# The last token tile of z moved behind the FFN's second inner product, and the first blocks of W loaded at the first free buffer

## The chip, the cores and the metric

The kernel runs on one core of a Trainium2 chip. The metric is device time in microseconds of one execution, and the median over runs is compared. The profile is of one such execution.

## The reference, cut to what matters

```python
# x: (2, 1024, 2048), ctx: (2, 2048, 2048), float32
def fake_quant(x, scale, zp):
    q = clip(round(x / scale + zp), 0, 255)
    return (q - zp) * scale

x = x + fake_quant(layernorm(x)) @ fake_quant(ctx[b])            # first layer, per batch b
z = layernorm(x)
x = x + z @ W + bias + LoRA(z)                                   # second layer, "the FFN"
# LoRA(z): a gated mixture of 16 adapters of rank 32, chosen per group of
# 256 tokens, and a shared adapter of rank 32: (z @ A_eff.T) @ B_eff.T + (z @ A_sh.T) @ B_sh.T
```

W is 2048 x 2048. Each of the 2 batches has 1024 tokens, that is 8 token tiles of 128 (m = 0 to 7), or 4 groups of 256 (g = 0 to 3).

## The kernel before, in words

**Stages.** The two batches are computed one after the other, and each has two stages: the first layer (called xattn here) and the FFN. The residual y (x, then the result) stays in SBUF, one tile of two token tiles per group.

**First layer.** Its product is made in pairs (n, g): 512 output columns n by one token group g. `xattn_pair` (line 555) issues 32 bf16 matmuls of 512 columns (line 530, tile `pa`). Then `end` (line 547) on VectorE scales the sums and adds them to y, and `bn_stats` (line 551) takes the statistics of the new y for the second layernorm. The last column block is n = 3: its four pairs (3, 0) to (3, 3) end the first layer of the batch.

**z.** When pair (3, g) is done, token tiles 2g and 2g+1 of y are complete, and `prep_z` (line 622) makes z of one tile. VectorE does a chain of small operations on 128 x 1 columns (lines 334 to 358, with one square root on ScalarE, line 341). Then for each half of 1024 columns VectorE writes (y - mean) * rstd into the buffer `wk` (line 628), TensorE transposes it in two groups of four 128 x 128 blocks into PSUM (line 632, tile `ptz`), and ScalarE copies each group into the z buffers (line 633). `wk` has one place for each half, so half h of tile m+1 can be written only when half h of tile m is transposed. `ptz` shares a PSUM pool of two buffers (`ps_m`) with other small tiles. `group_z` (line 635) does the two tiles of a group and then writes z to a scratch in DRAM (`zs`, line 639, issued on ScalarE's queue).

**LoRA's first product.** `lora_ax` (line 642) multiplies two groups' z by the adapters: 64 matmuls of 256 columns on TensorE (line 648, tile `px`). It comes once for groups 0 and 1 and once for groups 2 and 3. `Delta` (line 658) spreads the second LoRA product (line 694, tile `pl`) over the FFN.

**FFN.** z @ W is done by two levels of Strassen's method in Winograd's form: 7 outer combinations (o, table OUTER), and in each 7 inner products (s, table INNER). One inner product (`product`, line 812) is 8 float32 matmul instructions of 512 columns on 256 tokens; the profile records each of them as two rows. Their sums collect in the PSUM chains `fu`, `fv` and `fw`, and `spread` (line 837) adds a chain to y on VectorE (line 852). The operands are blocks of z (names a.., buffers `lit`) and of W (names b.., buffers `big`) and sums and differences of them. `comb` (line 766) makes these: those of W on VectorE as 128 x 2048 operations, those of z on GpSimd (POOL) as 128 x 1024 operations, both with line 771 in the profile. For o = 0 the combinations are t1 = b12 - b11, t2 = b22 - t1, t3 = b22 - b12, s1 = a21 + a22, s2 = s1 - a11, s3 = a11 - a21. The blocks a11, a12, a21, a22 of o = 0 are sums over two groups of z, done on VectorE at line 1093; a21 and a22 are written over the z of group 1, so they wait until `px` and the write to `zs` have read it.

**Buffers.** `big` has 9 buffers, handed out by a first-in first-out list while the program is built. They hold the first layer's operands (four `c1T` buffers, one for each group, and two pairs for ctx), `wk`, and in the FFN the blocks of W. A load of W (line 752, on SyncE's queue, 1 MB each) waits until its buffer is free.

**What sets the order.** The Tile framework orders the instructions of each engine when the kernel is built, by the program's order and its own estimates. So an FFN matmul can stand between two transposes where the data allow it. On the chip the order of each engine is fixed, and each engine runs its own list in order.

**Around the change** (lines 1068 to 1113): the operands of o = 0 are loaded one by one while pairs (3, 0) to (3, 3) run; `group_z` of a group stands after the next pair; `group_z` of group 3, `lora_ax` of groups 2 and 3, and `Delta` stand ahead of the first FFN product in the program.

Of the kernel before, what the change touches and what calls it, by code (L numbers as in the profile page):

```python
# [15 lines left out]
ALU = mybir.AluOpType  # L16
# [82 lines left out]
def tile_quant_xattn_then_lora_ffn(  # L99
# [17 lines left out]
    nc = tc.nc  # L117
    B, S, D = x.shape
    KT = D // P
    MT = S // P  # L120
# [8 lines left out]
    MG = GT // P  # L129
# [15 lines left out]
    big = Bufs([const.tile([P, KQ, NB], F32, tag=f"big{i}", name=f"big{i}") for i in range(9)])  # L145
    lit = Bufs([const.tile([P, KQ, GT], F32, tag=f"lit{i}", name=f"lit{i}") for i in range(10)])
# [13 lines left out]
    zs = [  # L160
        [[dram.tile([P, KQ, GT], F32, tag=f"zs{b}{g}{q}", name=f"zs{b}{g}{q}") for q in range(4)] for g in range(GPB)]
        for b in range(B)
    ]
# [89 lines left out]
    for i, s in enumerate((x1_scale, x1_zp, x2_scale, x2_zp)):  # L253
# [16 lines left out]
        out=gate_b.rearrange("p b n -> p (b n)"), in_=gate.rearrange("b n -> (b n)").partition_broadcast(P)  # L270
# [82 lines left out]
    def norm_stats(stats, name):  # L353

        mean, ve = variance(stats, name)
        r0, t = end_norm(ve, root_of(ve, name), name)
        rstd = small.tile([P, 1], F32, tag="rstd", name=f"rstd_{name}")
        nc.vector.tensor_mul(rstd, r0, t)
        return mean, rstd

    def halves(buf):

        f = flat(buf)
        return f[:, 0:H], f[:, H : 2 * H]
# [190 lines left out]
    def xattn_pair(b, n, g, c1T, c2):  # L555
        p = Pair(b, n, g, c1T, c2)
        for j in range(MG):
            with tc.high_priority():
                p.begin(j)
            p.products(j, range(KT))  # L560
        summed = p.end()
        p.stats()
        return summed
# [47 lines left out]
    def lora_b_step(b, n):  # L611

        st, sf = gated(f"b{b}_{n}")
        for c in range(NC):
            for i in range(2):
                nc.sync.dma_start(
                    out=bd[b][i::2, i, ds(c * RC, RC), ds(n * NB, NB)],
                    in_=sf[ds(c * GP + i * (GP // 2), GP // 2), :],
                )
        q2b.give(st)  # L620

    def prep_z(b, m, zq, wk):

        nm = f"{b}_{m}"
        g, tok = m // MG, ds((m % MG) * P, P)
        mean, rstd = norm_stats(st2[:, m], f"z{nm}")
        for h, t in enumerate(halves(wk)):
            nc.vector.tensor_scalar(t, y[g][:, m % MG, ds(h * H, H)], mean, rstd, ALU.subtract, ALU.mult)
            for u in range(2):
                pt = ps_m.tile([P, KQ, P], F32, tag="pm", name=f"ptz_{nm}_{h}_{u}")  # L630
                for k in range(KQ):
                    nc.tensor.transpose(pt[:, k, :], t[:, ds((4 * u + k) * P, P)], ident)  # L632
                nc.scalar.copy(zq[2 * h + u][:, :, tok], pt)

    def group_z(b, g, wk, zq):
        for j in range(MG):
            prep_z(b, g * MG + j, zq, wk)
        for q in range(4):
            nc.scalar.dma_start(out=zs[b][g][q], in_=zq[q])
        return zq  # L640

    def lora_ax(b, pr, zqs):

        px = ps_m.tile([P, GT], F32, tag="pm", name=f"px_{b}_{pr}")
        for k in range(KT):
            for i in range(2):
                g = 2 * pr + i
                nc.tensor.matmul(  # L648
                    px[i * 2 * R : (i + 1) * 2 * R, :],
                    acat[:, k, ds(3 * pr + i, 2), :].rearrange("p s r -> p (s r)"),  # L650
                    zqs[i][k // KQ][:, k % KQ, :],
                    start=(k == 0),
                    stop=(k == KT - 1),
                    skip_group_check=True,
                )
        nc.scalar.copy(axT[:, pr, :], px)
# [149 lines left out]
    def acc_tag(o, chain):  # L806

        return "delta" if chain == "v" and o > 3 else f"acc{(o + (chain != 'u')) % 2}"
# [3 lines left out]
    def product(b, o, s, ops, chains):  # L812

        an, bn, chain, opens, (i, j) = INNER[s]
        if opens:
            if chain == "u" and b + 1 == B and o == NO - 1:

                chains[chain] = [ps_m.tile([P, NB], F32, tag="pm", name=f"f{chain}_{b}_{o}{m}") for m in range(MG)]
            else:
                ps = ps_acc.tile([P, MG, NB], F32, tag=acc_tag(o, chain), name=f"f{chain}_{b}_{o}")  # L820
                chains[chain] = [ps[:, m, :] for m in range(MG)]
                whole[chain] = ps
        ps = chains[chain]
        ends = not any(c == chain and not op for _, _, c, op, _ in INNER[s + 1 :])
        at, bt = ops.t[an], ops.t[bn]
        for m in range(MG):
            for k in range(KQ):
                nc.tensor.matmul(  # L828
                    ps[m],
                    at[:, k, ds(m * P, P)],  # L830
                    bt[:, k, :],
                    start=(opens and k == 0),
                    stop=(ends and k == KQ - 1),
                    skip_group_check=True,
                )
# [17 lines left out]
            if done:  # L853
                nc.scalar.dma_start(out=out[b, ds(g * GT, GT), cols].rearrange("(j p) n -> p j n", p=P), in_=yp)

    def ffn(b, ops, meanwhile):

        delta = Delta(b)
        for o in range(NO):
            nxt = Operands(b, o + 1) if o + 1 < NO else None  # L860
            chains = {}
            for s in range(len(INNER)):
                product(b, o, s, ops, chains)
                if s in OWN:
                    OWN[s](ops)
                if nxt and s in AHEAD:
                    AHEAD[s](nxt)
                spread(b, o, s, chains)
                if s in (1, 4):
                    delta.step()  # L870
                added = line.last
                if nxt:
                    for name in BLOCKS.get(s, ()):
                        nxt.block(name)
                for name in DROP.get(s, ()):
                    ops.drop(name)
                if nxt:
                    for name in BEGIN.get(s, ()):
                        nxt.load(name)
                with tc.issue_after(added):  # L880
                    meanwhile(o, s)
            ops = nxt
# [20 lines left out]
    wk = big.take()  # L903
# [6 lines left out]
    def close_c2(n):  # L910
        for t in c2b.pop(n):
            big.give(t)
# [107 lines left out]
    for b in range(B):  # L1020
# [45 lines left out]
        close_c2(2)  # L1066
        bp.give(colt.pop(2))
        first = Operands(b, 0)
        first.load("b11")
        zqs = {}  # L1070
        for g in range(GPB):
            xattn_pair(b, 3, g, c1T, c2[3])
            big.give(c1T_bufs[g])
            if g == 0:
                first.block("b11")
                first.load("b12")
            elif g == 1:
                first.block("b12")
                first.comb("t1", "b12", "b11", ALU.subtract)
            elif g == 2:  # L1080
                first.load("b22")
            if g < 3:
                lora_b_step(b, g + 1)
            if g > 0:
                zqs[g - 1] = [lit.take() for _ in range(4)]
                group_z(b, g - 1, wk, zqs[g - 1])
            if g == 2:

                lora_ax(b, 0, [zqs[0], zqs[1]])
                for i in range(2):  # L1090
                    for j in range(2):
                        to = lit.take() if i == 0 else zqs[i][j]
                        nc.vector.tensor_add(to, zqs[i][j], zqs[i][2 + j])
                        first.t[f"a{i + 1}{j + 1}"] = to
                for t in (*zqs[0], *zqs[1][2:]):
                    lit.give(t)
        close_c2(3)
        bp.give(colt.pop(3))
        first.block("b22")
        z3 = [big.take() for _ in range(2)]  # L1100
        zqs[3] = [t[:, :, ds(h * GT, GT)] for t in z3 for h in range(2)]
        first.load("b21")
        group_z(b, 3, wk, zqs[3])
        big.give(wk)
        first.block("b21")
        first.comb("t2", "b22", "t1", ALU.subtract)
        first.comb("s1", "a21", "a22", ALU.add)
        first.comb("s2", "s1", "a11", ALU.subtract)
        lora_ax(b, 1, [zqs[2], zqs[3]])
        for t in zqs[2]:  # L1110
            lit.give(t)
        for t in z3:
            big.give(t)

        state = {"x": 0}

        def meanwhile(o, s):
# [41 lines left out]
            if s == len(INNER) - 1:  # L1159
# [5 lines left out]
                for m in range(4, MT):  # L1165
                    load_x(nb, m, slice(H, D))

        ffn(b, first, meanwhile)
        if b + 1 < B:
            c1T_bufs, c1T, wk = state["c1b"], state["c1T"], state["wk"]  # L1170

# [52 lines left out]
```

## Time and profile before

| | us |
|---|---|
| median of 3 runs (lowest to highest) | 1082.38 (1082.28 to 1082.62) |
| time of the profiled execution | 1082.56 |
| its span, first to last instruction | 1080.8 |
| TensorE (PE) busy | 1054.6 |
| VectorE (DVE) busy | 766.6 |
| ScalarE (ACT) busy | 247.4 |
| GpSimd (POOL) busy | 253.8 |

A row of the timeline has its start and its length in us, both on the profile's own clock, then the engine, the line of the code, the operation, the tile written and the tiles read, and in brackets the idle time of the engine just before it with what ended it. A row can merge several instructions (x8). The chain of waits lists the work that ended last, in order of time: start, length, what. In the first batch the last pair of the first layer ends at 179.5 us and the FFN runs until about 515 us. In the second batch the same pair ends at 708.1 us. The mean granted clock of TensorE is 1.00.

### The profile page before, as it was taken

The page shows a single profiled execution, that of the slowest core. Times are in us where ns is not written, and L with a number is a line of the kernel's source. Part 1 is how long each engine was busy: PE and PEld are TensorE (multiplying, and loading weights), DVE is VectorE, ACT ScalarE, POOL GpSimd, SP SyncE. Part 2 cuts the span into 40 slices and gives each one's busy share as a digit, 9 for nine tenths or more (in the row PEclk, how much of TensorE's full clock was granted, in tenths as well). Part 3 has the DMA queues.
Part 4 walks back from the last instruction along what each step waited for, and adds up shares of the span by engine and source line. Part 5 has one row for each costly group of instructions (what it writes and reads, how often), then busy time and mean ns, then how long its engine had stood idle before and what let it go on. Part 6 is the DMA issues. An engine that isn't in the chain of part 4 may idle for free.

```text
span 1080.8 us, 10609 instructions
## 1 busy us (share of the span) xinstructions
PE 1054.6 (98%) x3932; PEld 489.8 (45%) x3932; DVE 766.6 (71%) x949; ACT 247.4 (23%) x351; POOL 253.8 (23%) x104
## 2 busy tenths in 40 slices
PE   5999999999999999999999999999999999999998
PEld 2443345544444444444444444554444444444443
DVE  7986867578877676677859655674969667756851
ACT  5866133210000000001675741331000000000000
POOL 0000003032435302533000000032244531253600
PEclk9999999999999999999999999999999999999999
DMA  9979645788798476699673292559889874748611
GB/s 341 381 196 308 190 176 190 256 316 295 263 339 324 160 264 217 191 372 321 230 246 119 98 266 103 198 210 360 294 269 297 288 269 148 264 146 301 214 39 58
DMA packets 119228, 257.15 MB, mean 238 GB/s; under 512 B 11272, under 2 KB 15496, under 8 KB 118152
## 3 DMA queue, kind: packets, MB, share of 16 engines
q1 hardware_dynamic: 98688, 215.05, 58.4%
q10 hardware_dynamic: 20168, 40.38, 10.7%
q0 software_dynamic: 320, 1.05, 0.4%
q8 instruction: 31, 0.51, 0.2%
q14 instruction: 21, 0.17, 0.1%
HBM read 220.79 MB, written 37.75 MB: 239 GB/s over the span
## 4 chain that ended last, share of the span: by engine, by line
PE 83%; DVE 8%; DMA 4%; ACT 3%; issue 1%; SPq 0%; ACTq 0%
PE fu L828 34%; PE fv L828 17%; PE pa L530 12%; PE fw L828 9%; PE pl L694 3%; PE px L648 3%; PE ptz L632 2%; DMA lit<-in_ctx_dram 2%; DVE st L551 2%; DVE st L383 1%; ACT q2b L458 1%; DVE y L547 1%; ACT big L412 1%; DVE big L771 1%; PE pg_b L574 1%
## 5 line engine op out<-in xcount | busy, mean ns | idle before, releaser
L828 PE MATMUL fu<-big,lit 128*128 128x512 f32 x896 | 395.3, 593 | 0.0
L828 PEld LDWEIGHTS fu<-big,lit 128*128 128x128 f32 x896 | 168.6, 190 | 206.3 <-issue 204.9
L530 PE MATMUL pa<-big,big 128*128 128x512 bf16 x1024 | 237.1, 381 | 7.3 <-ACT pa L526 3.4
L771 POOL TENSOR_TENSOR lit<-lit,lit 128x1024 f32<-128x1024 f32 x56 | 164.7, 2950 | 189.7 <-PE fw L828 74.6
L828 PE MATMUL fv<-big,lit 128*128 128x512 f32 x448 | 197.9, 594 | 0.0
L771 DVE TENSOR_TENSOR big<-big,big 128x2048 f32<-128x2048 f32 x56 | 164.4, 2935 | 0.7
L530 PEld LDWEIGHTS <-big 128*128 128x128 bf16 x1024 | 97.1, 98 | 136.3 <-issue 29.6
L762 POOL TENSOR_TENSOR lit<-lit,lit 128x1024 f32<-128x1024 f32 x32 | 85.7, 2677 | 256.4 <-DMA lit<-zs 230.4
L852 DVE TENSOR_TENSOR y<-y,fu 128x1024 f32<-128x1024 f32 x92 | 108.5, 1215 | 40.6 <-PE fu L828 40.2
L828 PEld LDWEIGHTS fv<-big,lit 128*128 128x128 f32 x448 | 84.3, 190 | 105.0 <-issue 104.7
L458 ACT ACTIVATE q2b<-lit,sc,inv 128x1024 int16<-128x1024 f32 x64 | 76.4, 1232 | 163.7 <-DMA lit<-in_ctx_dram 147.1
L852 DVE TENSOR_TENSOR y<-y,fv 128x1024 f32<-128x1024 f32 x48 | 56.8, 1218 | 78.8 <-PE fv L828 78.8
L762 DVE TENSOR_TENSOR big<-big,big 128x2048 f32<-128x2048 f32 x40 | 101.8, 2546 | 0.0
L828 PE MATMUL fw<-big,lit 128*128 128x512 f32 x224 | 99.4, 592 | 0.0
L683 ACT COPY pl<-bias 128x1024 f32<-128x1024 f32 x16 | 16.3, 1018 | 294.1 <-DVE y L705 258.1
L679 POOL DMA_DIRECT2D bp<-bd x4 | 2.6, 660 | 344.3 <-DMA bd<-q2b 166.3
L852 DVE TENSOR_TENSOR y<-y,fw 128x1024 f32<-128x1024 f32 x24 | 28.4, 1218 | 53.9 <-PE fw L828 53.9
L828 PEld LDWEIGHTS fw<-big,lit 128*128 128x128 f32 x224 | 42.1, 190 | 50.7 <-issue 50.7
L547 DVE SCALAR_TENSOR_TENSOR y<-pa,k_s,y 128x1024 f32<-128x1024 f32 x32 | 41.0, 1280 | 32.2 <-PE pa L530 32.1
L526 ACT ACTIVATE pa<-bp,r_s 128x512 f32<-128x512 f32 x58 | 39.0, 685 | 87.0 <-PE pa L530 57.1
L705 DVE TENSOR_TENSOR y<-pl,y 128x512 f32<-128x512 f32 x64 | 39.8, 679 | 17.5 <-PE pl L694 17.2
L383 DVE BATCH_NORM_STATS2 st<-y 128x6 f32<-128x512 f32 x64 | 41.4, 679 | 5.7 <-DMA y<-in_x_dram 5.6
(93 smaller groups left out, 629.6 us busy)
## 6 DMA issues: line engine op xcount, KB each, us to landing
big<-in_w_dram SPq DMA_DIRECT2D x96, 1024.0 KB
lit<-zs SPq DMA_DIRECT2D x80, 512.0 KB
lit<-in_ctx_dram SPq DMA_DIRECT2D x64, 512.0 KB
out_dram<-y ACTq DMA_DIRECT2D x30, 512.0 KB
zs<-lit ACTq DMA_DIRECT2D x24, 512.0 KB
lit<-in_lora_a_dram SPq DMA_DIRECT2D x32, 256.0 KB
lit<-in_lora_bt_dram SPq DMA_DIRECT2D x32, 256.0 KB
y<-in_x_dram SPq DMA_DIRECT2D x16, 512.0 KB
```

The source lines that it names most:

```text
L383: nc.vector.bn_stats(st1[:, self.m, n, :], self.y[:, ds(n * NB, NB)])
L458: nc.scalar.activation(qi, t, AF.Relu, bias=z2, scale=inv2)
L526: nc.scalar.activation(self.pa[:, j, :], colt[self.n], AF.Identity, bias=r_s[:, m : m + 1])
L530: nc.tensor.matmul(self.pa[:, j, :], self.c1T[:, k, ds(j * P, P)], self.c2[k // 8][:, k % 8, :], start=not self.begun[j], stop=(k == KT - ...
L547: return nc.vector.scalar_tensor_tensor(yp, self.pa, s12, yp, ALU.mult, ALU.add)
L648: nc.tensor.matmul(px[i * 2 * R : (i + 1) * 2 * R, :], acat[:, k, ds(3 * pr + i, 2), :].rearrange("p s r -> p (s r)"), zqs[i][k // KQ][:, ...
L694: nc.tensor.matmul(pl[j][i][:, half], axT[rows, pr, ds(j * P, P)], bt[rows, half], start=False, stop=True, skip_group_check=True,)
L705: line(nc.vector.tensor_add(yb, pl[j][i], yb))
L762: line(eng.tensor_tensor(got[0], got[0], got[1], ALU.add if terms[1][2] > 0 else ALU.subtract))
L771: line(eng.tensor_tensor(out_t, at[p], at[q], op))
L828: nc.tensor.matmul(ps[m], at[:, k, ds(m * P, P)], bt[:, k, :], start=(opens and k == 0), stop=(ends and k == KQ - 1), skip_group_check=True,)
L852: line(nc.vector.tensor_tensor(yp, yp, whole[chain], op))
```

## The change

In the program's order, three things change.

1. Before, the four W blocks of o = 0 were loaded as b11 ahead of pair (3, 0), b12 after it, b22 after pair (3, 2) and b21 after the last pair. Now b11 and b12 are loaded ahead of pair (3, 0), b22 after it and b21 after pair (3, 1). t1 is made after pair (3, 2) instead of after pair (3, 1).
2. Of group 3, only tile 6 is normalised and transposed ahead of the FFN. Tile 7, the write of group 3 to `zs`, and `lora_ax` of groups 2 and 3 are now in a function `last_z`.
3. The FFN's inner product s = 1 of o = 0 (`fw`, a12 times b21) is issued directly after s = 0, and then `last_z` and `Delta`, ahead of the other work of step s = 0.

No instruction is added or removed on TensorE, ScalarE, GpSimd or SyncE, and none of VectorE's operations.

```diff
-    def ffn(b, ops, meanwhile):
-        delta = Delta(b)
+    def ffn(b, ops, meanwhile, last_z):
         for o in range(NO):
             nxt = Operands(b, o + 1) if o + 1 < NO else None
             chains = {}
             for s in range(len(INNER)):
-                product(b, o, s, ops, chains)
+                if (o, s) != (0, 1):
+                    product(b, o, s, ops, chains)
+                if (o, s) == (0, 0):
+                    product(b, o, 1, ops, chains)
+                    last_z()
+                    delta = Delta(b)
                 if s in OWN:
                     OWN[s](ops)
...
         first = Operands(b, 0)
-        first.load("b11")
+        for name in ("b11", "b12"):
+            first.load(name)
+            first.block(name)
         zqs = {}
         for g in range(GPB):
             xattn_pair(b, 3, g, c1T, c2[3])
             big.give(c1T_bufs[g])
-            if g == 0:
-                first.block("b11")
-                first.load("b12")
-            elif g == 1:
-                first.block("b12")
-                first.comb("t1", "b12", "b11", ALU.subtract)
-            elif g == 2:
-                first.load("b22")
+            if g < 2:
+                name = ("b22", "b21")[g]
+                first.load(name)
+                first.block(name)
...
                 for t in (*zqs[0], *zqs[1][2:]):
                     lit.give(t)
+                first.comb("t1", "b12", "b11", ALU.subtract)
         close_c2(3)
         bp.give(colt.pop(3))
-        first.block("b22")
         z3 = [big.take() for _ in range(2)]
         zqs[3] = [t[:, :, ds(h * GT, GT)] for t in z3 for h in range(2)]
-        first.load("b21")
-        group_z(b, 3, wk, zqs[3])
-        big.give(wk)
-        first.block("b21")
+        for j in range(MG - 1):
+            prep_z(b, 3 * MG + j, zqs[3], wk)
         first.comb("t2", "b22", "t1", ALU.subtract)
         first.comb("s1", "a21", "a22", ALU.add)
         first.comb("s2", "s1", "a11", ALU.subtract)
-        lora_ax(b, 1, [zqs[2], zqs[3]])
-        for t in zqs[2]:
-            lit.give(t)
-        for t in z3:
-            big.give(t)
+        def last_z():
+            prep_z(b, MT - 1, zqs[3], wk)
+            big.give(wk)
+            for q in range(4):
+                nc.scalar.dma_start(out=zs[b][3][q], in_=zqs[3][q])
+            lora_ax(b, 1, [zqs[2], zqs[3]])
+            for t in zqs[2]:
+                lit.give(t)
+            for t in z3:
+                big.give(t)
```

## The prediction, made before the changed kernel ran

> **What bounds the kernel now.** I read the busy shares first, then the chain of waits around the two changed places, then the timelines of VectorE and GpSimd there.
>
> ```profile
> PE 1054.6 (98%) x3932; PEld 489.8 (45%) x3932; DVE 766.6 (71%) x949; ACT 247.4 (23%) x351; POOL 253.8 (23%) x104
> ```
>
> TensorE works for 98% of the span, so the change can only gain or lose by TensorE's idle time where the first layer passes into the FFN. I count that stretch from the first FFN row among the last pair's rows (163.53 us in batch 0, 692.04 in batch 1) to the end of the second `px` (209.68 and 736.52): 46.15 and 44.48 us. The chain of waits in batch 0:
>
> ```profile
> 163.53 0.86 PE fu L828 x2
> ...
> 171.45 7.06 PE px L648 x64
> 178.51 0.98 PE pa L530 x4
> ...
> 184.94 4.07 DVE big L771
> 189.01 0.12 DVE ve_z L336 x2
> 189.13 2.20 DVE big L771
> 191.33 2.26 DVE y L852 x2
> ...
> 195.30 1.06 PE ptz L632 x8
> 196.37 0.86 PE fw L828 x2
> 197.23 0.87 PE ptz L632 x8
> ...
> 201.57 1.06 PE pl L694 x6
> 202.62 7.06 PE px L648 x64
> ```
>
> See here that the transposes of tiles 6 and 7 already alternate with `fw` rows, and that VectorE carries the path from 184.94 to 195.30. The work of a stretch, by such rows: 8 `fu` and 8 `fw` matmuls at 0.86 (13.7), 16 `pa` at 0.22 (3.5), 12 half tiles of transposes at 0.87 (10.4), two `px` at 7.06 (14.1), `pl` 1.06: 42.9 us. TensorE therefore loses 3.3 us in batch 0 and 1.6 in batch 1. **4.9 us is the most that the change can gain.**
>
> **How VectorE and GpSimd share.** The timeline of the same places, VectorE and GpSimd:
>
> ```profile
> 178.96 2.36 POOL L771 TENSOR_TENSOR lit<-lit,lit 128x1024 f32<-128x1024 f32 x1 [10.72 <-DMA zs<-lit]
> 180.72 1.16 DVE L628 TENSOR_SCALAR big<-y,mv_z,rstd_z 128x1024 f32<-128x1024 f32 x1
> 183.00 1.65 DVE L628 TENSOR_SCALAR big<-y,mv_z,rstd_z 128x1024 f32<-128x1024 f32 x1
> 184.06 2.80 POOL L771 TENSOR_TENSOR lit<-lit,lit 128x1024 f32<-128x1024 f32 x1
> 184.86 4.14 DVE L771 TENSOR_TENSOR big<-big,big 128x2048 f32<-128x2048 f32 x1
> ...
> 228.25 3.30 DVE L762 TENSOR_TENSOR big<-big,big 128x2048 f32<-128x2048 f32 x1
> 229.37 4.40 POOL L771 TENSOR_TENSOR lit<-lit,lit 128x1024 f32<-128x1024 f32 x1
> 231.59 4.32 DVE L771 TENSOR_TENSOR big<-big,big 128x2048 f32<-128x2048 f32 x1
> ```
>
> GpSimd's operation of 178.96 ends at 181.32; VectorE's 0.8 us operation (line 628), begun at 180.72, ends 0.56 us later. GpSimd's last one ends at 186.86 and VectorE's combination, begun at 184.86, ends 2.14 us later. They exclude each other, and they take turns: GpSimd's operation of 229.37 ends 2.22 us after VectorE's (231.55), and VectorE's next, asked for at 231.59, ends 2.14 us after GpSimd's (233.77). So beside GpSimd's three operations s1, s3, s2 (2.2 to 2.4 us each) every line 628 or 771 on VectorE waits for one of them. `bn_stats` and line 547 don't: at 179.52 and 181.80 they took their usual 1.28 and 1.27.
>
> **What moves.** The same instructions run. The built order shows on TensorE hardly a change: 12 half tiles still alternate with FFN rows; in batch 0 the last 4 `pa` now come before `px`, not after it, and one matmul of the third inner product stands ahead of the second `px` (I take its 0.86 off below). On VectorE more moves. (a) t1 goes from the pairs before to between tiles 2 and 3. (b) In batch 0, tiles 4 and 5 were normalised under `px`, before the last pair ended; now t2, the sums a21 and a22, the last pair's statistics and 11 small operations stand first, and t3 stands between tiles 4 and 5. (c) In batch 1, a21 and a22 now stand ahead of tile 4. They wait for `px`, and GpSimd's s1 is released by the same `px`, so tile 4 meets GpSimd.
>
> **Batch 0, in order.** Up to 167.28 (tile 2 transposed) nothing differs. Then 7 `pa` (1.51), half a tile (0.87), one `pa`, half a tile with its eviction wait (1.12), 5 `pa`: the last pair ends at 172.1. t1's 2.14 hide under the 7 `pa`. TensorE goes on: one `fu` to 172.96, `px` to 180.0, `fu` to 180.9, and then wants tile 4.
> VectorE from 172.1: line 547 (1.2) and t2 (2.2) to 175.5, a21 1.15, a22 not before `px` has read its second quarter (in batch 1 3.70 after its start: 176.66) to 177.8, statistics 1.2, small operations 1.3 (8 of them took 0.83 at 193.52): 180.3. GpSimd's s1 starts 5.42 after `px` (705.27 less 699.85): 178.4, to 180.75. So:
> - Tile 4, first half: written at 181.3 behind s1. TensorE waits 0.5.
> - Second half: s3 has its turn, 181.3 to 183.55, so 184.1. TensorE, ready at 183.15, waits 1.05.
> - t3 comes next; s2 has its turn to 186.35, t3 ends at 188.5, tile 5's first half is there at 189.3. TensorE has been ready since 185.95: 3.4.
> - After that nothing is late (tile 6 is written by 191.8, wanted at 193.7). From 190.25 the remaining 14.9 us and `px` end at 213.05; less 0.86, 212.2, against 209.68: **+2.5 us**.
>
> **Batch 1.** `px` starts at 699.95 with 3 more `pa` done than before (a gain of 0.55). TensorE wants tile 4 at 707.45. a22 starts at 703.65, the small operations end at 705.65. s1 starts at 705.37, so GpSimd is first by 0.28. Tile 4's first half is written at 708.3 (TensorE waits 0.95), its second at 711.1 behind s3 (1.05), line 547 then runs to 712.3, tile 5's first half comes at 713.85 behind s2 (1.05), its second at 715.9 (0.3). Tile 6 follows 8.5 us later, as before, under 7.7 us of FFN rows and a half tile. The end less 0.86 is 738.8, against 736.52: **+2.3 us**.
>
> **Costed at nothing.** The earlier W loads: no row shows TensorE waiting for W (`fw` starts at 189.13 on the heels of `fu`), so their gain is nothing. On SyncE's in-order queue b22 and b21 now stand ahead of LoRA's writes to `bd` and wait for a pair to end, some 8 us; `bd` is first read by a load issued at 153.78 and needed by `pl` at 201.5, so 40 us cover that. On ScalarE tile 7's square root now waits behind `px`'s copy, at 180, needed at 190. `Delta`, the `zs` writes and the second `px` end no later than the stretch itself. Each would cost its own lateness, a few us, if that cover went. From the stretch's end to the kernel's end only TensorE's order counts, so both losses reach the end.
>
> **Sum.** 1082.56 (the profiled run, span 1080.8 and 1.8 around it; 0.18 over the median) + 4.8 = 1087.3.
>
> **A price I leave out.** TensorE's wait of 3.4 us has no equal late in this trace. After the wait of 1.72 at 195.30 the next rows keep their pace (0.87). After the 8.01 at 13.14, 4 bf16 matmuls took 1.89 us at 16.39, and later 36 took 7.95. Between these ends the cost is nothing to some 2 us; 3.4 is nearer to 1.72, so I take nothing. [...]
>
> **Rivals.**
> - *Won race* (0.13). In batch 1 tile 4 reaches the lock before s1; I have it lose by 0.28. Then tile 4 is in time, and waits of 1.05 and 1.1 stay: 1.15 less lost, 1086.1. For it: the margin is small. Against: a22 may also wait for its `zs` write, which makes it later.
> - *No turns* (0.16). VectorE keeps the lock for operations that follow each other at once. Against it: the rows at 229.37 and 231.59. Then tile 4 is whole at 182.1, t3 at 184.4, and batch 0 loses 0.4 + 0.5, ending 1.5 us earlier than before, while batch 1 loses 1.0: 1082.1, which is no slower. The same time comes if the change does nothing, since the transposes lay among FFN rows already.
> - *The waits go* (0.09), faster. This is what taking VectorE's chain off the path would do: tile 6's wait of 1.72 goes, as t2 is made early, and tiles 4 and 5 are ready when TensorE wants them. It decides by whether tile 5's first half is written before 184.2 and 710.9. Only the eviction waits ahead of `px` (1.0 in each stretch) stay: 4.9 - 2.0, so 1079.7. For it: in batch 0 the wait at 195.30 does go by my count. Against it: the turns.
>
> **Numbers.** My forecast has 0.62: 1087.3, within it 1085 to 1089.6 (the clock's price above, and waits half as long below). About 0.2%, 2.2 us, is what can be told from no change. Slower: forecast and won race, 0.75; same: no turns, 0.16; faster: 0.09. The range goes from 1081.8 to 1089.6, so that it takes in the no-turns case.
>
> **What would show it.** Right: no wait at tile 6 in batch 0; TensorE idle before `ptz` of tiles 4 and 5 in both batches, put down to line 628, about 5 and 3 us; VectorE's t3 at 4 us or more beside GpSimd's third operation in batch 0. Wrong: line 628 at 0.8 us for tile 4, or no idle TensorE before tile 5, or other idle time in the passage from batch 0's FFN into batch 1, which I hold unchanged.

## The result, and the profile after

| | before | after |
|---|---|---|
| median of 4 runs each, on one chip (lowest to highest), us | 1082.5 (1082.28 to 1082.88) | 1095.17 (1093.65 to 1096.1) |
| profiled execution, us | 1082.56 | 1094.92 |
| its span, us | 1080.8 | 1093.1 |
| mean granted clock of TensorE | 1.00 | 0.995 |

The ratio is 1.0115 (95% interval 1.0098 to 1.0133). The change is slower, as forecast, but it loses 12.3 us and not 4.8; 1095.17 lies above the range. The busy shares of after:

```profile
PE 1058.0 (97%) x3900; PEld 494.2 (45%) x3932; DVE 774.0 (71%) x949; ACT 247.9 (23%) x351; POOL 245.3 (22%) x104
```

TensorE's busy time rises by only 3.4 us, so most of the 12.3 us between the spans is idle time. The place is found by the end of the second `px`. It ends at 217.14 in batch 0 and at 749.72 in batch 1, against 209.68 and 736.52. One FFN matmul (0.86) now stands ahead of it. Without it the changed kernel is 6.6 us behind at the first mark and 12.3 behind at the second, which is the whole difference of the spans: **6.6 us in batch 0, 5.7 us in batch 1**, where 2.5 and 2.3 were forecast. The chain of waits of after, batch 0, with the second `px` of both batches at its end:

```profile
172.09 0.86 PE fu L828 x2
172.95 1.90 PE px L648 x16
...
179.36 1.52 DVE nt_z L349 x2
...
181.07 2.10 DVE rstd_z L358
183.16 0.17 DVE mv_z L334
183.34 2.12 DVE rstd_z L358
185.46 0.74 DVE big L628
186.20 0.14 issue
186.33 1.94 PE ptz L632 x8
188.27 1.71 PE fu L828 x2
189.98 1.66 PE ptz L632 x8
191.64 0.86 PE fu L828 x2
192.50 0.88 PE ptz L632 x8
...
210.08 7.06 PE px L648 x64
...
742.66 7.06 PE px L648 x64
```

Two things are new here. Line 358 writes 128 numbers (128 x 1) and takes 2.1 us. And behind the wait, `ptz` and `fu` take twice their time (1.7 to 1.9, later 0.86 to 0.88). The timeline of VectorE and GpSimd (POOL) in the same place, and of batch 1, shows the first:

```profile
178.38 7.07 POOL L771 TENSOR_TENSOR lit<-lit,lit 128x1024 f32<-128x1024 f32 x3 [7.49 <-PE px L648]
179.28 1.60 DVE L349 SCALAR_TENSOR_TENSOR nt_z<-ve_z,r_z 128x1 f32<-128x1 f32 x2
180.80 0.14 DVE L350 TENSOR_SCALAR nt_z<-nt_z 128x1 f32<-128x1 f32 x1
...
180.99 2.18 DVE L358 TENSOR_TENSOR rstd_z<-r_z,nt_z 128x1 f32<-128x1 f32 x1
183.26 2.20 DVE L358 TENSOR_TENSOR rstd_z<-r_z,nt_z 128x1 f32<-128x1 f32 x1
185.38 1.53 DVE L628 TENSOR_SCALAR big<-y,mv_z,rstd_z 128x1024 f32<-128x1024 f32 x2
...
712.21 7.52 POOL L771 TENSOR_TENSOR lit<-lit,lit 128x1024 f32<-128x1024 f32 x3 [6.55 <-DVE nt_z L349]
712.28 2.37 DVE L358 TENSOR_TENSOR rstd_z<-r_z,nt_z 128x1 f32<-128x1 f32 x2
714.61 5.67 DVE L628 TENSOR_SCALAR big<-y,mv_z,rstd_z 128x1024 f32<-128x1024 f32 x2
717.67 1.94 PE L632 MATMUL ptz<-ident,big 128*128 128x128 f32 x8 [3.29 <-DVE big L628]
```

Small operations with two tensors (lines 349 and 358), 0.15 to 0.22 us each from 192.41 on, where GpSimd is still, take up to 2.2 us while GpSimd runs. Those with one tensor (line 350) stay at 0.14 in the midst of it. So in batch 0 the three of GpSimd's operations are passed one by one: by line 349, by the first and by the second line 358, and tile 4 is written when GpSimd has ended. In batch 1 line 358 passes the first of them, and the two halves of line 628 (5.67 us) pass the other two. TensorE waits 5.27 us for tile 4 in batch 0 and 3.29 in batch 1. The second finding is in the windows of after; the eighth column (PEclk, behind the five engines' busy times) is the granted clock:

```profile
182.00:184.00 2.00, 0.00 (x0) 0.00 (x0) 2.00 (x3) 0.00 (x0) 2.00 (x2) 1.00 0.00 0
184.00:186.00 2.00, 0.00 (x0) 0.00 (x0) 2.00 (x2) 0.00 (x0) 1.45 (x1) 0.66 0.00 0
186.00:188.00 2.00, 1.67 (x8) 1.70 (x9) 2.00 (x5) 0.75 (x2) 0.00 (x0) 0.50 0.00 0
190.00:192.00 2.00, 2.00 (x10) 1.76 (x10) 0.32 (x1) 0.91 (x2) 0.00 (x0) 0.63 0.00 0
```

In batch 0 it falls to 0.50 in the midst of the wait, and stays there until 191.5.

### The profile page after: what moved, and what is told of

It reads as the page before. It is cut to its first block, busy times and chain, and to the rows that moved or that the text cites. A ratio compares the mean times of both kernels' runs of the same rounds, so it can differ in the third digit from the quotient of the medians.

```text
span 1093.1 us, 10587 instructions
## 1 busy us (share of the span) xinstructions
PE 1058.0 (97%) x3900; PEld 494.2 (45%) x3932; DVE 774.0 (71%) x949; ACT 247.9 (23%) x351; POOL 245.3 (22%) x104
## 3 DMA queue, kind: packets, MB, share of 16 engines
q0 software_dynamic: 320, 1.05, 0.4%
## 4 chain that ended last, share of the span: by engine, by line
PE 83%; DVE 8%; DMA 4%; ACT 3%; issue 2%; SPq 0%; ACTq 0%; DVEq 0%
PE fu L828 35%; PE fv L828 17%; PE pa L530 12%; PE fw L828 9%; PE pl L694 3%; PE ptz L632 3%; DMA lit<-in_ctx_dram 2%; PE px L648 2%; DVE st L551 1%; DVE st L383 1%; ACT q2b L458 1%; DVE y L547 1%; ACT big L412 1%; PE pg_b L574 1%; PE pg_a L574 1%
## 5 line engine op out<-in xcount | busy, mean ns | idle before, releaser
L530 PE MATMUL pa<-big,big 128*128 128x512 bf16 x992 | 232.8, 381 | 8.7 <-ACT pa L526 3.3
L771 POOL TENSOR_TENSOR lit<-lit,lit 128x1024 f32<-128x1024 f32 x56 | 161.8, 2897 | 198.8 <-PE fw L828 94.4
L762 POOL TENSOR_TENSOR lit<-lit,lit 128x1024 f32<-128x1024 f32 x32 | 80.4, 2514 | 265.2 <-DMA lit<-zs 239.5
L705 DVE TENSOR_TENSOR y<-pl,y 128x512 f32<-128x512 f32 x64 | 40.0, 681 | 21.8 <-PE pl L694 21.1
L632 PE MATMUL ptz<-ident,big 128*128 128x128 f32 x256 | 37.0, 291 | 9.4 <-DVE big L628 8.6
```

What stands on the lines that cost most here:

```text
L530: nc.tensor.matmul(self.pa[:, j, :], self.c1T[:, k, ds(j * P, P)], self.c2[k // 8][:, k % 8, :], start=not self.begun[j], stop=(k == KT - ...
L705: line(nc.vector.tensor_add(yb, pl[j][i], yb))
L762: line(eng.tensor_tensor(got[0], got[0], got[1], ALU.add if terms[1][2] > 0 else ALU.subtract))
L771: line(eng.tensor_tensor(out_t, at[p], at[q], op))
```

## The experiments

**Theory** after the two traces: the change puts t1, the two sums and in batch 0 also t2 ahead of tile 4's operations on VectorE. Tile 4 therefore meets GpSimd's s1, s3 and s2, and every VectorE operation with two tensors waits there for one of them. The idle time that follows also halves TensorE's clock (0.50 in the windows above). **Rivals**: the loss comes from the moved tile 7 and the reordered products (parts 2 and 3); or from the early W loads as transfers; or GpSimd is only beside the point. In the listings of variants the line numbers move by a few. "Before" is run again beside each group: 1083.46, 1083.4, 1083.57 and 1082.65 us in the four groups, the last of them on another chip.

### GpSimd later

```diff
+ # for o = 0, GpSimd's s1 and s3 also wait for tile 6's last line 628
+ if self.o == 0 and name in ("s1", "s3"):
+     tc.add_manual_dep(made.ins, held[6].ins.name, ...)
```

> The changed kernel, with GpSimd's s1, s3 and s2 held until tile 6's second half is written; everything else keeps its place. Theory (GpSimd's three operations block VectorE's chain for tile 4, and the idle time halves TensorE's clock): tile 4 is written near 181 in batch 0 and near 706 plus the shift in batch 1, no TensorE wait over 1 us, the granted clock stays 1.00, time 1079.5 to 1083. Rival (VectorE's new order, t2 and the sums ahead of tile 4, makes it late by itself): 1088 or more.

Measured: 1083.15 us, ratio 0.999 (0.9975 to 1.0006), clock 1.0. This is 0.15 us above the expected 1079.5 to 1083, and otherwise as the theory has it: with nothing else altered the whole loss is gone as soon as GpSimd is out of the way. In its trace the same small operations take 0.10 to 0.28, and TensorE does not wait for tile 4:

```profile
179.78 0.15 DVE L358 TENSOR_TENSOR rstd_z<-r_z,nt_z 128x1 f32<-128x1 f32 x1
181.01 1.04 PE L634 MATMUL ptz<-ident,big 128*128 128x128 f32 x8
```

What it gains over before at tile 6, it pays at tile 7 of batch 1, which now meets GpSimd (line 628 twice, 5.37 us; TensorE waits 0.61).

### The small operations with one tensor each

```diff
-        r0, t = end_norm(ve, root_of(ve, name), name)
-        nc.vector.tensor_mul(rstd, r0, t)
...
+        nc.vector.reciprocal(r0, sd)
...
+        nc.vector.tensor_scalar(t, ve, r0, r0, ALU.mult, ALU.mult)
+        nc.vector.tensor_scalar(t, t, -0.5, 1.5, ALU.mult, ALU.add)
...
+        nc.vector.tensor_scalar(rstd, r0, t, 1.0, ALU.mult, ALU.mult)
```

> The changed kernel, with the two 128 x 1 operations that read two tensors (lines 349 and 358) written as operations that read one tensor and take the others as scalars. GpSimd stays. Theory (only operations with two tensor inputs, however small, and line 628 and 771 wait for GpSimd): the small operations take 0.15 us beside GpSimd, tile 4 waits for one GpSimd operation and no more, t3 for another, so the prediction's own account holds: 1085 to 1090. Rival (any VectorE operation waits there, or they wait for ScalarE's roots): no better than 1093.

Measured: 1093.1 us, ratio 1.0074 (1.0051 to 1.0097). The size was missed (1085 to 1090 was expected), and this run is the most telling of all. The timeline:

```profile
180.48 0.33 DVE L363 TENSOR_SCALAR rstd_z<-r_z,nt_z 128x1 f32<-128x1 f32 x2
180.73 4.04 DVE L633 TENSOR_SCALAR big<-y,mv_z,rstd_z 128x1024 f32<-128x1024 f32 x2
184.92 4.21 DVE L776 TENSOR_TENSOR big<-big,big 128x2048 f32<-128x2048 f32 x1
190.00 1.94 PE L637 MATMUL ptz<-ident,big 128*128 128x128 f32 x8 [3.17 <-DVE big L633]
```

The small operations no longer wait (0.33 for two, beside GpSimd). But the turns are not gone, others take them: the two halves of tile 4 (4.04 instead of 1.5) and t3 (4.21). TensorE waits 0.37, 0.84 and 3.17 us in batch 0, and its clock is at 0.50 from 189.1 to 195.9. The waits are those of the prediction (0.5, 1.05 and 3.4) within 0.25 us, as the table in the next section shows in another way; the half clock comes on top. So about 3 us of the loss went with the small operations, and 9.6 us against the kernel before, run beside it, remain.

### Part 1 alone, and parts 2 and 3 alone

Part 1 alone is before with the first group of edits: the loads and the place of t1. Parts 2 and 3 alone is after with these taken back.

```diff
 # part 1 alone, against before
+        for name in ("b11", "b12"):
+            first.load(name)
+            first.block(name)
...
+                first.comb("t1", "b12", "b11", ALU.subtract)
 # parts 2 and 3 alone, against after
-            if g < 2:
-                name = ("b22", "b21")[g]
...
+            elif g == 1:
+                first.block("b12")
+                first.comb("t1", "b12", "b11", ALU.subtract)
```

> The kernel before, with part 1 alone: W's four blocks loaded early and t1 made after pair (3, 2). Theory (the new place of t1, t2 and t3 in VectorE's order does the damage): VectorE's order around tiles 4 and 5 is that of the changed kernel, so 1092 to 1097. Rival (moving tile 7 and the second px behind the FFN's products does it): 1081 to 1084.

> The changed kernel, with W loaded and t1 made where they were before: parts 2 and 3 alone. Theory: VectorE's order around tiles 4 and 5 is the old one, so 1080.5 to 1083.5. Rival (parts 2 and 3 do it): 1092 to 1097.

Measured: part 1 alone 1093.61 us, ratio 1.0081 (1.0054 to 1.0109); parts 2 and 3 alone 1085.42 us, ratio 1.0012 (0.9998 to 1.0027). The timeline of TensorE with part 1 alone has the same two waits as after, to the hundredth:

```profile
187.70 1.94 PE L632 MATMUL ptz<-ident,big 128*128 128x128 f32 x8 [5.27 <-DVE big L628]
718.56 1.67 PE L632 MATMUL ptz<-ident,big 128*128 128x128 f32 x8 [3.29 <-DVE big L628]
```

So part 1 does most of the damage (10.2 us), by its loads or by its t1. Parts 2 and 3 alone came out some 2 us above the 1080.5 to 1083.5 that I had expected, and by medians as much above the kernel before, though the interval takes in no change. In that order t2 still stands beside GpSimd (4.27 us), and tile 6's wait stays, so nothing is gained there:

```profile
196.33 1.06 PE L632 MATMUL ptz<-ident,big 128*128 128x128 f32 x8 [1.83 <-DVE big L628]
```

And from the start of the first `px` to the end of the second, less the one FFN matmul, its trace takes 1.0 us more than before in each batch. This is the third step of the next section, seen without part 1.

### t1 in another place

```diff
-                first.comb("t1", "b12", "b11", ALU.subtract)      # ahead of the last group
...
+        first.comb("t1", "b12", "b11", ALU.subtract)
         first.comb("t2", "b22", "t1", ALU.subtract)
```

> The changed kernel with one statement moved: t1 stands directly ahead of t2, not ahead of the last group. W is still loaded early. In the built order tile 4's small operations and its normalisation come ahead of t1 and of the two sums on VectorE, as in the kernel before. Theory (the place of t1 ahead of tile 4 pushes tile 4 under GpSimd's three operations, and that is the whole loss): tile 4 is ready when px ends, no idle time of 3 us or more before ptz, clock 1.0, time 1081 to 1084.5. Rival (the early W loads themselves, by their transfers or by what they hold up on SyncE, cost some of it): 1087 or more.

Measured: 1082.96 us, ratio 1.0003 (0.9988 to 1.0018). The early W loads stay, one statement is moved, and the loss is gone. In the built order tile 4's small operations and its normalisation now stand ahead of t1, t2 and the two sums, as they stood ahead of t2 and the sums in before. Here t1 ends under the first `px`, and `ptz` of tile 4 follows the last `pa` without a wait:

```profile
170.49 2.29 DVE L771 TENSOR_TENSOR big<-big,big 128x2048 f32<-128x2048 f32 x1
179.10 1.04 PE L632 MATMUL ptz<-ident,big 128*128 128x128 f32 x8
```

So it is neither the loads nor their transfers: it is **the place of t1**, which in the built order drags tile 4 behind t1, t2, the two sums and the last pair's statistics in batch 0, and behind t1 and the two sums in batch 1.

### GpSimd's operations in halves

```diff
+ for k in range(0, KQ, KQ // 2):          # s1, s2, s3 of o = 0 in two halves, 128x512 each
+     ks = slice(k, k + KQ // 2)
+     line(eng.tensor_tensor(out_t[:, ks, :], at[p][:, ks, :], at[q][:, ks, :], op))
```

> The changed kernel with GpSimd's s1, s3 and s2 of the first layer-2 product each made in two halves (128x512, about 1.2 us each). Theory (a VectorE operation that meets GpSimd waits for the one GpSimd operation that runs, and they take turns): the 128x1 operations of lines 349 and 358 then take 1.1 to 1.4 us instead of 2.2, tile 4's first half is written 2 us earlier, the wait before ptz in batch 0 falls from 5.27 to 2.5 to 3.5 us, and the time is 1088 to 1092. Rival (VectorE is stopped until GpSimd's whole string has ended): nothing shortens, 1094 to 1096.

Measured: 1092.19 us, ratio 1.0082 (1.0062 to 1.0102); just above the expected 1088 to 1092. Its timeline:

```profile
178.59 8.54 POOL L774 TENSOR_TENSOR lit<-lit,lit 128x512 f32<-128x512 f32 x6 [8.07 <-DVE lit L1100]
181.34 1.11 DVE L358 TENSOR_TENSOR rstd_z<-r_z,nt_z 128x1 f32<-128x1 f32 x1
182.56 3.44 DVE L628 TENSOR_SCALAR big<-y,mv_z,rstd_z 128x1024 f32<-128x1024 f32 x2
184.47 1.94 PE L632 MATMUL ptz<-ident,big 128*128 128x128 f32 x8 [2.85 <-DVE big L628]
```

Line 358 waits half as long (1.11 for 2.18) as GpSimd's operation is half as long (8.54 us for six, where after had 7.07 for three): in both traces the wait is about **one operation of GpSimd**, and that for a VectorE operation of 128 x 1. But there are now six turns, so line 628 pays too (3.44 for two halves, where after had 1.53). In batch 1 both of line 349 wait (2.54 together) and TensorE's wait is 3.11, hardly less than 3.29. So cutting GpSimd's work finer helped here where two small operations waited (TensorE's wait in batch 0 fell from 5.27 to 2.85), and hardly in batch 1, where line 628 still took 3.40 for two halves.

### TensorE kept busy

```diff
+        for _ in range(32 if pr == 0 else 0):      # adds zeros to px
+            nc.tensor.matmul(px, zeros_h, ones_h[:, 0:1].to_broadcast([P, GT]), start=False, ...)
```

> The changed kernel with 32 matmuls on zeros (some 3.5 us, bf16, 128x256) put behind the first px of each batch, adding zeros to the same sums, so that TensorE works through most of the idle time in which it waits for tile 4. Theory: of the 12.3 us lost, 2.7 (batch 0) and 1.4 (batch 1) are the rows after the wait, which ran at a granted clock of 0.5; with the fill the clock stays at 1.0, the ptz row after the wait takes 1.04 and not 1.94, and the time is 1089.5 to 1092.5. The waits themselves stay. Rival (the slow rows have another cause than the idle time, or the fill only lengthens TensorE's work): 1094.5 or more, with the row still at 1.9.

Measured: 1096.95 us, ratio 1.0122 (1.0102 to 1.0142). The expectation (1089.5 to 1092.5) fell, in two ways. In batch 0 the fill took the place of the `fu` row, and 2.67 us of idle time were left behind it; the clock fell again (0.50 from 186.2 to 193.0).

```profile
186.71 1.09 PE L632 MATMUL ptz<-ident,big 128*128 128x128 f32 x4 [2.67 <-DVE big L628]
```

In batch 1 there was no idle time and the clock stayed at 1.0 (`ptz` 1.04), but nothing was gained: TensorE then waited 0.78 us for the next half and 0.74 for an eviction, which in after it had spent in slow rows. So half clock in front of a wait costs little here. That it costs in full where no wait follows, as in batch 0 of after, is read from the rows alone.

### The clock by itself

```diff
+ # before, in batch 0 only: line 628 of tile 6's first half made n + 1 times
+ for _ in range(n + 1 if (b, m, h) == (0, 6, 0) else 1):
      nc.vector.tensor_scalar(t, y[g][...], mean, rstd, ALU.subtract, ALU.mult)
```

> The kernel before, with the normalisation of the first half of tile 6 (line 628) made twice in batch 0 alone, so that TensorE's wait of 1.72 us there becomes some 2.45. Nothing else moves. Theory (an idle time of TensorE costs its length and, from a length between 1.8 and 2.7 us, half clock for the next 3.4 or 6.8 us): either 0.7 us slower than before with the clock at 1.0, or 2.1 to 3.6 us slower with rows of 1.94; it tells where the length begins. Rival (the clock's fall in the changed kernel came with GpSimd's and VectorE's clash and not with the idle time): 0.7 us slower, clock 1.0.

> The kernel before, with the same normalisation made four times in batch 0, so that TensorE's wait there becomes some 3.9 us. Theory: the wait costs 2.2 us and the clock falls to 0.5 for 3.4 or 6.8 us after it began to fall, which costs 1.4 to 2.9 us more: 3.6 to 5.1 us slower than before, ptz behind the wait at 1.9. Rival (as for the run with one repeat): 2.2 us slower, ptz behind the wait at 1.06, clock 1.0.

Measured: with one repeat 1084.59 us, ratio 1.0005 (0.9994 to 1.0017); with three 1090.36, ratio 1.0045 (1.0023 to 1.0066). The framework put more `fw` rows ahead of tile 6 in both, so the wait came to 1.46 us with one repeat (no fall of the clock) and 3.55 with three, where 2.45 and 3.9 were meant:

```profile
202.56 1.94 PE L633 MATMUL ptz<-ident,big 128*128 128x128 f32 x8 [3.55 <-DVE big L629]
208.63 1.97 PE L633 MATMUL ptz<-ident,big 128*128 128x128 f32 x8
```

With three repeats the clock was at 0.50 from 200.9 to 211.1, and the loss is 6.8 us by medians where 3.6 to 5.1 were expected. One of the repeats also met a fourth operation of GpSimd, which lengthened the wait. The clash of the two engines is not what makes the clock fall, since the kernel before has it too (t2 at 4.14) and keeps its clock behind a wait of 1.72; in the profiles it is the length of the idle time that parts the two. The ten runs with three repeats fall into two groups: three with a mean clock of 0.999 to 1.0 took 1083.0 to 1084.7 us, the seven with 0.995 to 0.997 took 1088.3 to 1091.8. This is not the price of the clock alone: 10.2 us at half clock cost 5.1 at most, an estimate from rows such as `ptz` (1.94 and 1.97 there, 1.04 at a clock of 1.00), and the medians of the groups lie 7.3 apart, so something else was shorter in the three as well, most likely the wait. No trace of them tells.

### A version that beats both

> The kernel with t1 late (tile 4 ahead of t1 on VectorE) and with GpSimd's s1 and s3 also held back until tile 6's z is written, so that GpSimd meets neither tiles 4 to 6 nor t2 and t3. Theory: no VectorE operation between the pairs and tile 6 takes longer than alone, tile 6's wait of 1.72 us of the kernel before goes too; of the 4.9 us that could be gained at most, the eviction waits of 1.0 in each batch and what GpSimd's later start costs at tile 7 (0.6 in batch 1 of the earlier run) stay: 1079.5 to 1082 where the kernel before takes 1082.5 to 1083.5. Rival (what holds up the second px is not GpSimd's place, so that nothing is to be gained): 1082.5 or more.

> The kernel before, with GpSimd's s1 and s3 held back until tile 7's z is written, behind all that VectorE does for the tiles. Theory: t2 beside GpSimd falls from 4.1 to 2.2 us, TensorE's wait of 1.72 us before tile 6 goes, lines 628 of tiles 4 and 5 no longer wait, and s2 (about 7 us after tile 7) is still there ahead of the third inner product, since the second px lies between: 0.8 to 1.8 us faster than before. Rival (s2 or s3 comes late for the third or fourth inner product, or what is gained is lost at the next wait): no difference or slower.

> The changed kernel with t1 late and with GpSimd's s1 and s3 held back until tile 7's z is written, as in the run of the kernel before with that hold (1080.95). It tells whether the rest of the change, tile 7 behind the second inner product, is worth anything once GpSimd meets none of the tiles. Theory: no tile waits, but in this order a row of the third inner product, which needs s2, stands ahead of the second px; s2 comes some 4.8 us after tile 7 is written, about 1 us late: 1081 to 1083, no better than the hold in the kernel before. Rival (tile 7 behind the second product does bring its own gain, and s2 is in time): 1080 or less.

The first is the change with t1 late and GpSimd held behind tile 6; the second is the kernel before with GpSimd held behind tile 7 (the edit of the first experiment, with `held[7]`); the third is the change with t1 late and s1, s2 moved behind tile 7 with the same hold. Measured: 1083.38 us, ratio 1.0001 (0.9991 to 1.001); **1080.95 us, ratio 0.997 (0.9955 to 0.9984)**; 1082.93 us, ratio 1.0002 (0.9993 to 1.001). The first missed its 1079.5 to 1082. The second gained more than the 0.8 to 1.8 us expected, 2.6 by medians and 2.0 between the spans of the two traces. The third came as expected. The timeline of the second:

```profile
184.22 2.23 DVE L773 TENSOR_TENSOR big<-big,big 128x2048 f32<-128x2048 f32 x1
193.70 1.04 PE L634 MATMUL ptz<-ident,big 128*128 128x128 f32 x8
197.47 9.44 POOL L773 TENSOR_TENSOR lit<-lit,lit 128x1024 f32<-128x1024 f32 x4 [28.64 <-DVE big L630]
```

t2 takes 2.23 instead of 4.14, tile 6 (193.70) no longer waits, and s2 and s3 are in time because the second `px` covers them. In the first of the three, tile 7 meets the delayed GpSimd in both batches (TensorE waits 0.61 and 0.62). In the third no tile waits, but a `fu` row ahead of the second `px` waits 0.54 us for s2, and the end of the stretch is longer in the new order (see the next section). So with GpSimd out of the way, parts 2 and 3 are not worth anything; in the second run no wait of TensorE for VectorE or GpSimd is left there for them to fill.

## Why the prediction was right in sign and wrong in size

**Right.** What moves on VectorE, and the start of the stretch: the last pair was put at 172.1 and `px` at 172.96, and they came at 172.09 and 172.95. GpSimd's s1 was put at 178.4 and came at 178.38. Tile 6's wait went. TensorE's waits stand before `ptz` of tile 4 and are put down to line 628. VectorE and GpSimd take turns (1.60, 2.18 and 2.20 us on VectorE beside GpSimd's three operations of batch 0). The earlier W loads themselves cost nothing (1082.96 with them and t1 late, 1083.4 before). The bound of 4.9 us on the gain was not put to the test by a loss; the best run gained 2.6.

**The step that failed: "small operations 1.3" and 0.83.** I priced the 128 x 1 operations by a row where GpSimd was still, and my list of what waits held only lines 628 and 771. But lines 349 and 358 read two tensors each. In batch 0 those that waited took 1.60, 2.18 and 2.20 us, 6.0 where 1.3 stood for all eleven; in batch 1 line 358 took 2.37. The run without such operations tests the rest of the ledger. TensorE's start on a tile, in us from the start of the first `px`:

| | predicted | after | small operations with one tensor |
|---|---|---|---|
| batch 0, tile 4 | 8.4 | 13.5 | 8.6 |
| batch 0, tile 5 | 16.4 | 19.5 | 16.4 |
| batch 1, tile 4 | 8.5 | 11.0 | 8.6 |
| batch 1, tile 5 | 13.9 | 16.4 | 14.1 |

With that one term mended, all four come within 0.2 us. The time does not: 1093.1 is still far above 1087.3, so this step alone is not the miss. In after each turn taken by a small operation is a turn that line 628 or t3 doesn't take, since GpSimd has only three: that is why t3 took 2.28 and not the "4 us or more" that I had named, and why the wait that I put before tile 5 in batch 0 (3.4) came before tile 4.

**The second step: "so I take nothing" for the clock.** I reasoned from the row at 195.30 (a wait of 1.72 with no fall) for a wait of 3.4. All nine waits of 2.67 us or more that the profiles show in these stretches (after 2, one tensor 1, part 1 alone 2, halves 2, fill 1, three repeats 1) were followed by a clock of 0.50; the four of 1.42 to 1.83 were not. That such a wait always does it is not shown: of the five runs with one-tensor operations one has a mean clock of 1.0 (1091.23 us), and no trace tells its wait. In batch 0 of after, tile 5's first half was written at 189.95 and TensorE came to it at 192.50: 2.55 us. In batch 1 the slow rows lie ahead of a wait for VectorE and cost about nothing. No run shows the clock's price that the range's upper end, 1089.6, takes in; what the rows of after show in its place is these 2.55 us in batch 0 and about nothing in batch 1.

**The third, small:** in both batches the rows behind tile 5 took about 1 us more than I had counted. Two `pl` rows (0.63) now stand ahead of the second `px`, and the eight behind it took 1.88 us where before had 1.13, so this isn't given back. The rest is 0.15 at the last half tile, which waits for an eviction (1.02 where others take 0.87), and 0.19 at the FFN row behind it (1.05 for 0.86).

The sum: 12.3 = 4.8 predicted + 0.65 (tile 5 late in batch 0) + 2.55 (clock) + 2.5 (tile 5 late in batch 1) + 1.9 (rows behind), which gives 12.4. Not all of the 2.5 is turns: tile 5's first half was written at 722.20 in batch 1, and TensorE started on it at 723.09. An FFN row ran until about 722.7, and then TensorE waited 0.37 us for an eviction that ScalarE made only after copying a `pl` tile (line 683, 1.02 us at 721.51). So the mis-sized turns account for about 2.3 of the 7.5 missing, this delay for 0.9, the clock for 2.55, and the rows behind tile 5 for 1.9. The clock's share shows in no run by itself; it is read from the rows. Of the rivals, "no turns" and "the waits go" are excluded by the rows; "won race" asked whether tile 4 reaches GpSimd's turn before s1, and the race was lost one step earlier, at line 358 (712.28 against 712.21).

## What to carry to other kernels

Before moving VectorE's work under GpSimd's, list the VectorE operations of the kinds that waited here: those with two tensors, down to 128 x 1 (lines 349 and 358, up to 2.2 us for 0.15 to 0.22; line 771, 4.14 in before for 2.23 with GpSimd held), and the large one with one tensor (line 628, 5.67 for 1.53 in two halves). Charge each with one whole operation of GpSimd (2.2 to 2.4 us here); then ask how many such operations GpSimd has (three here), since in each batch of after three of VectorE's waited, and no more. A wait of TensorE as long as the nine of 2.67 to 5.27 us here should be charged with half clock behind it as well, where no other wait follows (2.55 us in batch 0 of after). And where both engines feed a third, the cheap remedy is to start the one that is not urgent later: here that made the kernel before 0.3% faster, by making s1 and s3 wait for tile 7.

## What the runs showed of the hardware that was not expected

- In these profiles the granted clock falls and rises on a beat of 3.41 us. Windows of 0.2 us, each with its mean clock, place the two falls of after at 184.64 and 717.12, those of the run with halves at 184.45 and 716.92, those with part 1 alone at 186.39 and 718.87. The stretches at 0.50 lasted 3.41 us (batch 1 of after), 6.83 us (batch 0 of after) and 10.24 us (three repeats): one, two and three times 3.41. Each pair of falls is 532.5 us apart, 156 times a third of the 10.24, while the waits of a pair end 531.3 us apart (after, 186.33 and 717.67), 531.4 (halves) and 530.9 (part 1 alone). The fall can even come behind the wait: with halves, batch 1, the wait ended at 715.84 and the clock fell at 716.92. Nor was TensorE idle for a whole beat ahead of each fall: in the run with the fill, matmuls ran until 184.04 and the clock fell at 186.17, so the 3.41 us ahead of the fall held 1.3 us of matmuls.
- At the kernel's start the recorded clock does not say how fast TensorE ran. Before waits 8.01 us there at a clock of 1.00, and parts 2 and 3 alone has 0.50 from 7.5 to 21.1. But the four matmuls at 16.39 (before) and at 16.92 (parts 2 and 3 alone) took the same 1.89 us in both, where four of them take 1.04 at 178.44 in before:

```profile
16.39 1.89 PE L530 MATMUL pa<-big,big 128*128 128x512 bf16 x4 [2.22 <-DVE big L428]
16.92 1.89 PE L530 MATMUL pa<-big,big 128*128 128x512 bf16 x4 [2.21 <-DVE big L428]
```

  So both ran at about half pace there, and only one record says so. A run's mean clock of 0.993 against 1.00 can come from this alone (13.6 of 1083.8 us at 0.50 take 0.006 off the mean); it need not mean a slower run: of parts 2 and 3 alone, the runs at 0.993 and 0.994 took 1084.6 to 1085.57 us, those at 1.0 took 1083.74 to 1087.06.
- A 128 x 1 operation of 0.15 us cost 2.2 us here (line 358), and the same arithmetic with scalar operands took 0.33 for two beside GpSimd. Line 628, with one tensor too but 128 x 1024, does wait (4.04 for two halves in that run, 1.52 behind GpSimd). Which condition parts the two, no run here shows.
- Clock and VectorE waits hide one another: taking the fall away in batch 1 (fill) left the time as long as it was: 35.89 us from the start of the first `px` to that of the second, 35.88 in after.
